# A graph-attention layer on one core: scores and values in 64x64 array tiles, step by step, with a byte mask

## The chip, the cores and the metric

One Trainium2 chip, one core of it. The metric is the device time of one launch in microseconds (us), the median of several runs; less is better. The kernel of before takes 2929.03 us (three runs, 2928.76 to 2929.57).

## What is computed

Eight batches of 2048 nodes with 64 features, one adjacency matrix (2048x2048, int32) for all of them. Cut to what matters:

```
mask = adj + eye(N) > 0
h    = einsum('bnc,hdc->bhnd', x, Wh)                  # 4 heads of 64
def gat(h, b):
    s = where(mask, h @ h^T, -1e16)
    return softmax(s) @ h + b
z    = leaky_relu(concat of heads of gat(h, bh), 0.2)
h2   = z @ Wo^T                                        # back to 64
z2   = leaky_relu(gat(h2, bo), 0.2)
out  = layernorm(x + layernorm(z2) * gamma + beta)
```

All is float32. The kernel takes no maximum: it subtracts one constant shift before the exponential, and a flag computed from all denominators at the end says whether a general version must run again.

## The kernel before

**Units, chunks and steps.** Two attentions run side by side on the 128 partitions: two heads of one batch (a first unit: batch pair `bp`, batch `b2`, head pair `hp`), or the second attention of two batches (a second unit). There are 16 first and 4 second units. A unit is cut into 4 chunks `c` of W = 512 query columns, and a chunk into 16 steps `m`, one for each block of 128 nodes: 20 x 4 x 16 = 1280 steps, 80 chunks.

**One step.** `scores` (L525) makes two matmuls, one for each of the two heads `j`, each with 64 rows and 128 columns of the array (64 features in, 128 nodes out) on 512 columns, into one tile `s` of 128x1024 in PSUM. VectorE (DVE in the rows) subtracts the mask into SBUF (L532), ScalarE (ACT) takes the exponential in place (L534). `values` (L537) makes two more matmuls, each with 128 rows and 64 columns (128 nodes in, 64 features out), which accumulate over the 16 steps into one PSUM bank `o`. GpSimd (POOL) adds the exponentials of steps 0 to 12 into `acc` (`add_up`, L544), and the last three (`DIRECT = 3`) go to TensorE as they are. All matmuls are float32; each shows in the trace as two MATMUL records, its two passes.

**The end of a chunk.** `sums` (L559) adds `acc` and the three direct tiles over the partitions by matmuls with a matrix of ones (`pz`, four array tiles of 32 columns), ScalarE copies the result (`zsb`, L572), DMAs turn it (`zt`), and ScalarE and VectorE apply the leaky ReLU (L582, L583). `invert` (L586) makes the reciprocals on VectorE and spreads them by DMAs (`rd`, `z`), `scale` (L598) multiplies, and `project` (L601) multiplies by Wo (L608) or, in a second unit, by a centring matrix (L616), after which `norm1` and `norm2` (L631, L643) do both normalisations, mostly on VectorE in PSUM.

**The start of a unit.** `prepare` (L498) projects x into `hT` (`ph`, L510; K = 64 rows, 128 columns, one batch at a time) and transposes it into `hN` (`pn`, L520).

**The order.** Every engine runs its instructions in the order in which the program is written. It is written in periods of four steps (`BATCH = 4`): first the four `scores` of a period, then the four `values` of the period before, then the four `add_up`, then the jobs that have been put at this period (`at`, L674). The mask is built in the first periods by 32 jobs (`mask_job`, L682: load, turn into 0 or 1e16 in bf16, transpose, copy).

**Buffers.** PSUM has 8 banks: three score tiles of two banks (`psum`, bufs = 3; the tiles of `pz`, `ph`, `pn` and the mask turn in the same three) and two banks for `o`. There are 14 slots for exponentials and raw loads.

Of the kernel before, what the change touches and what calls it, by code (L numbers as in the profile page):

```python
# [29 lines left out]
BF16 = mybir.dt.bfloat16  # L30
AF = mybir.ActivationFunctionType
# [8 lines left out]
BIG = 1e16  # L40
# [313 lines left out]
def fast_kernel(ctx: ExitStack, tc: tile.TileContext, x, adj, Wh, bh, Wo, bo, gamma, beta, out, flag):  # L354
# [10 lines left out]
    BATCH = 4  # L365
    K = 2 * CB
    DIRECT = 3
# [3 lines left out]
    epool = ctx.enter_context(tc.tile_pool(name="epool", bufs=14))  # L371
    accs = ctx.enter_context(tc.tile_pool(name="accs", bufs=2))
    work = ctx.enter_context(tc.tile_pool(name="work", bufs=7))
    small = ctx.enter_context(tc.tile_pool(name="small", bufs=4))
    psum = ctx.enter_context(tc.tile_pool(name="psum", bufs=3, space=bass.MemoryType.PSUM))
# [9 lines left out]
    def opsum(name):  # L385
        return psum.tile([P, W], F32, tag="o", name=name, bufs=2)

    def wtile(name):
        return work.tile([P, W], F32, tag="w", name=name)

# [5 lines left out]
    identi = const.tile([P, P], I32, name="identi")  # L396
    nc.vector.tensor_copy(identi, ident)
# [21 lines left out]
    zall = const.tile([P, chunks, 8], F32, name="zall")  # L419

# [33 lines left out]

    mask = [const.tile([P, NB, W], BF16, name=f"mask{c}") for c in range(NC)]

# [6 lines left out]
    def mask_rows(c, g, st):  # L463
        if g // 2 == c:
            for k in range(2):
                r = 2 * (g % 2) + k
                d = st[:, r, k * P:(k + 1) * P]
                nc.gpsimd.tensor_tensor(d, d, identi, OP.add)
        m = work.tile([P, CB, 2 * P], BF16, tag="w", name=f"mrow{c}_{g}")
        nc.scalar.activation(m, st, AF.Relu, bias=shifts[:, 2:3], scale=-BIG)  # L470
        return m
# [15 lines left out]

    h2T = {}

    class Unit:  # L490
# [7 lines left out]
        def prepare(self, part):  # L498

            n, h = self.n, part % 2  # L500
            if part < 2:
                if self.second:
                    self.hT = h2T[self.bp]
                    return
                if h == 0:
                    self.hT = big.tile([P, N], F32, tag="hT", name=f"hT{n}")
                rows = slice(self.b2 * C, (self.b2 + 1) * C)
                p = spsum(f"ph{n}_{h}")
                for q in range(2):
                    nc.tensor.matmul(p[:, q * W:(q + 1) * W], whT[rows, self.hp * P:(self.hp + 1) * P],  # L510
                                     xT[self.bp][rows, (2 * h + q) * W:(2 * h + q + 1) * W], start=True, stop=True)
                nc.scalar.copy(self.hT[:, h * 1024:(h + 1) * 1024], p)  # L512
                return

            if h == 0:
                self.hN = big.tile([P, NB, P], F32, tag="hN", name=f"hN{n}")
            p = spsum(f"pn{n}_{h}")
            for k in range(NB // 2):
                m = h * NB // 2 + k
                nc.tensor.transpose(p[:, k * P:(k + 1) * P], self.hT[:, m * P:(m + 1) * P], ident)  # L520
            b = bob.rearrange("p r d -> p (r d)") if self.second else bhb[:, self.hp * P:(self.hp + 1) * P]
            nc.vector.tensor_add(self.hN[:, h * NB // 2:(h + 1) * NB // 2, :], p.rearrange("p (m d) -> p m d", d=P),  # L522
                                 b.unsqueeze(1).to_broadcast([P, NB // 2, P]))

        def scores(self, c, m):  # L525
            ps = spsum(f"s{self.n}_{c}_{m}")
# [10 lines left out]
        def values(self, c, m, e):  # L537
            if m == 0:
                self.O[c] = opsum(f"o{self.n}_{c}")
            for j in range(2):  # L540
                nc.tensor.matmul(self.O[c][j * D:(j + 1) * D, :], self.hN[:, m, j * D:(j + 1) * D], e[:, j, :],  # L541
                                 start=(m == 0), stop=(m == NB - 1))

        def add_up(self, c, m, e):  # L544
# [7 lines left out]
            elif m < NB - DIRECT:  # L552
# [4 lines left out]


        def sums(self, c):  # L559
# [20 lines left out]

            o5 = wtile(f"o5{n}_{c}")
            nc.scalar.mul(o5, self.O[c], SLOPE)  # L582
            nc.vector.tensor_tensor(self.O[c], self.O[c], o5, OP.max)  # L583
            self.zt[c] = zt

        def invert(self, c):  # L586
# [7 lines left out]
            self.z[c] = wtile(f"z{n}_{c}")  # L594
# [3 lines left out]
        def scale(self, c):  # L598
            nc.vector.tensor_tensor(self.z[c], self.O[c], self.z[c], OP.mult)  # L599

        def project(self, c):  # L601

            z, p = self.z[c], self.O[c]
            if not self.second:
                if self.bp not in h2T:
                    h2T[self.bp] = big.tile([P, N], F32, tag="h2T", name=f"h2T{self.bp}")
                rows = slice(self.b2 * D, (self.b2 + 1) * D)
                nc.tensor.matmul(p[rows, :], woT[:, self.hp, :], z, start=True, stop=True)  # L608
                dst = h2T[self.bp][rows, c * W:(c + 1) * W]
                if self.hp == 0:  # L610
                    nc.scalar.copy(dst, p[rows, :])
                else:
                    nc.vector.tensor_add(dst, dst, p[rows, :])  # L613
                return
            for i in range(CB):
                nc.tensor.matmul(p[:, i * P:(i + 1) * P], z[:, i * P:(i + 1) * P],  # L616
                                 centre.rearrange("p r d -> p (r d)"), start=True, stop=True)
            self.norm1(c, p.rearrange("p (k d) -> p k d", d=D))

        def rstd(self, c, y, tag):  # L620

            n = self.n
            st = small.tile([P, 2, K], F32, tag="st", name=f"st{n}_{c}_{tag}")
            sq = wtile(f"sq{n}_{c}_{tag}").rearrange("p (k d) -> p k d", d=D)
            nc.scalar.square(sq, y)  # L625
            nc.vector.tensor_reduce(st[:, 0, :], sq, AX.X, OP.add)  # L626
            nc.scalar.activation(st[:, 1, :], st[:, 0, :], AF.Identity, bias=shifts[:, 3:4], scale=1.0 / D)  # L627
            nc.gpsimd.tensor_tensor(st[:, 0, :], st[:, 1, :], mhalf, OP.pow)  # L628
            return st[:, 0, :].unsqueeze(2).to_broadcast([P, K, D])

        def norm1(self, c, y):  # L631
            xr = wtile(f"xr{self.n}_{c}")
            xv = xr.rearrange("p (i b d) -> p i b d", b=2, d=D)
            for b2 in range(2):
                nc.sync.dma_start(out=xv[:, :, b2, :],
                                  in_=x[2 * self.bp + b2, c * W:(c + 1) * W, :].rearrange("(i p) d -> p i d", p=P))
            nc.vector.tensor_mul(y, y, self.rstd(c, y, 0))
            nc.vector.tensor_mul(y, y, gam.unsqueeze(1).to_broadcast([P, K, D]))
            nc.vector.tensor_add(y, y, bet.unsqueeze(1).to_broadcast([P, K, D]))
            nc.vector.tensor_add(y, y, xr.rearrange("p (k d) -> p k d", d=D))  # L640
            self.xr = xr

        def norm2(self, c):  # L643
            if not self.second:
                return
            y = self.O[c].rearrange("p (k d) -> p k d", d=D)
            mu = small.tile([P, 2, K], F32, tag="mu", name=f"mu{self.n}_{c}")
            nc.vector.tensor_reduce(mu[:, 0, :], y, AX.X, OP.add)
            nc.scalar.mul(mu[:, 1, :], mu[:, 0, :], -1.0 / D)
            nc.vector.tensor_add(y, y, mu[:, 1, :].unsqueeze(2).to_broadcast([P, K, D]))  # L650
            r = self.rstd(c, y, 1)
            nc.vector.tensor_mul(self.xr.rearrange("p (k d) -> p k d", d=D), y, r)
            yv = self.xr.rearrange("p (i b d) -> p i b d", b=2, d=D)
            for b2 in range(2):
                nc.sync.dma_start(out=out[2 * self.bp + b2, c * W:(c + 1) * W, :].rearrange("(i p) d -> p i d", p=P),
                                  in_=yv[:, :, b2, :])
# [3 lines left out]
    for bp in range(B // 2):  # L660
        firsts = [(bp, b2, hp) for b2 in range(2) for hp in range(HP)]
# [6 lines left out]

    PER = NB // BATCH
    periods = [(u, c, q) for u in units for c in range(NC) for q in range(PER)]  # L670
    total = len(periods)
# [24 lines left out]
    for part in range(2):  # L696
        units[0].prepare(part)
# [3 lines left out]
    for part in range(2, 4):  # L701
        units[0].prepare(part)
# [95 lines left out]
```

## Time and profile before

| what | us |
|---|---|
| median of three runs | 2929.03 |
| the profiled execution, its own time | 2929.27 |
| its span in the trace | 2927.8 |
| TensorE busy, share of the span | 2730.6 (93%) |
| GpSimd busy | 2331.8 (80%) |
| VectorE busy | 1799.2 (61%) |
| ScalarE busy | 1656.4 (57%) |
| granted TensorE clock, mean | 0.977 of full speed |

The trace records each instruction with its engine, line and tiles. A busy time of TensorE is not TensorE at its peak: matmuls overlap each other, in different array tiles above all, so how fast it goes is read from the distance of the starts, in the timeline. A row of a timeline merges neighbours of one group: the start, the time from the first start to the last end, and the count; a number in brackets is the idle time ahead of it and what ended it.

### The profile page before, as it was taken

What the parts mean: (1) busy time and instruction counts of PE and PEld (TensorE: products, weight loads), DVE (VectorE), ACT (ScalarE), POOL (GpSimd) and SP (SyncE); (2) the same over time, 40 slices, a digit from 0 to 9 for tenths busy, and PEclk for the clock granted to TensorE, in tenths of its full rate; (3) what the DMA queues carried; (4) which work ended last, traced back from release to release, by engine and by line L of the source; (5) the groups of instructions that cost most, each with busy time, mean ns of one, the idle gap of its engine ahead of it and who ended that gap; (6) DMA issues with size and microseconds to landing.
All of it is one profiled execution on the core that took longest, in us unless ns stands there. A gap on an engine that the chain in (4) does not pass through costs nothing.

```text
span 2927.8 us, 33405 instructions
## 1 busy us (share of the span) xinstructions
PE 2730.6 (93%) x12550; PEld 967.9 (33%) x12550; DVE 1799.2 (61%) x1861; ACT 1656.4 (57%) x1625; POOL 2331.8 (80%) x1025
## 2 busy tenths in 40 slices
PE   7999999999998999999998899999999999998884
PEld 3333333333332333333333233333333333333221
DVE  4666656666666666566666665666566666666564
ACT  5765556556554555655654555565565556555442
POOL 5778888788777887888876888888888888877774
PEclk9999999999999999999999999999999999999997
DMA  4300001000000000100000000010000000000001
GB/s 129 123 16 8 8 8 26 8 8 8 12 22 17 10 9 8 23 8 8 12 18 12 19 8 9 8 26 8 8 8 8 8 8 12 8 12 23 15 19 27
DMA packets 118220, 54.03 MB, mean 18 GB/s; under 512 B 91266, under 2 KB 107714, under 8 KB 118050
## 3 DMA queue, kind: packets, MB, share of 16 engines
q1 hardware_dynamic: 117250, 51.36, 6.6%
q8 instruction: 100, 1.64, 0.2%
q0 software_dynamic: 176, 0.26, 0.1%
q14 instruction: 70, 0.57, 0.1%
q10 hardware_dynamic: 624, 0.20, 0.0%
HBM read 46.60 MB, written 4.52 MB: 17 GB/s over the span
## 4 chain that ended last, share of the span: by engine, by line
PE 60%; ACT 14%; DVE 11%; DMA 5%; issue 4%; SPq 3%; POOL 2%; ACTq 0%; DVEq 0%; POOLq 0%
PE o L541 28%; PE s L529 25%; ACT e L534 11%; DVE e L532 6%; DMA zt<-zsb 4%; SPq L578 3%; PE ph L510 2%; PE o L608 2%; POOL st L628 2%; ACT zsb L572 1%; PE pn L520 1%; ACT o L582 1%; PE pz L569 1%; DVE hN L522 1%; DVE st L626 1%
## 5 line engine op out<-in xcount | busy, mean ns | idle before, releaser
L554 POOL TENSOR_TENSOR acc<-acc,e 128x1024 f32<-128x1024 f32 x880 | 2079.9, 2363 | 79.5 <-ACT e L534 13.0
L534 ACT ACTIVATE e<-e,shifts 128x1024 f32<-128x1024 f32 x1280 | 1452.9, 1149 | 1034.3 <-DVE e L532 1024.6
L532 DVE TENSOR_TENSOR e<-s,mask 128x1024 f32<-128x1024 f32 x1280 | 1475.6, 1215 | 348.2 <-PE s L529 333.0
L541 PE MATMUL o<-e,hN 128*64 128x512 f32 x5120 | 1188.4, 607 | 0.0
L529 PE MATMUL s<-hT 64*128 64x512 f32 x4096 | 1004.3, 609 | 65.7 <-DVE e L532 65.7
L541 PEld LDWEIGHTS o<-e,hN 128*64 128x64 f32 x5120 | 343.5, 138 | 821.3 <-issue 600.9
L529 PEld LDWEIGHTS s<-hT 64*128 64x128 f32 x4096 | 384.1, 187 | 612.0 <-issue 308.0
L550 POOL TENSOR_TENSOR acc<-e,e 128x1024 f32<-128x1024 f32 x80 | 189.8, 2372 | 313.4 <-ACT e L534 313.4
L529 PE MATMUL s<-h2T 64*128 64x512 f32 x1024 | 261.6, 634 | 68.8 <-DVE e L532 50.6
L628 POOL TENSOR_TENSOR st<-st,mhalf 128x8 f32<-128x8 f32 x32 | 52.7, 1647 | 179.2 <-ACT st L627 179.2
L529 PEld LDWEIGHTS s<-h2T 64*128 64x128 f32 x1024 | 95.0, 192 | 215.3 <-DVE e L532 92.2
L583 DVE TENSOR_TENSOR o<-o,o 128x512 f32<-128x512 f32 x80 | 56.0, 700 | 175.8 <-ACT o L582 175.8
L569 PE MATMUL pz<-e,ones 128*32 128x512 f32 x960 | 154.1, 601 | 0.0
L589 DVE TENSOR_REDUCE zall<-zt 128x8 f32<-128x16 f32 x80 | 13.7, 171 | 199.1 <-DMA zt<-zsb 199.0
L569 PE MATMUL pz<-acc,ones 128*32 128x512 f32 x320 | 84.7, 600 | 6.2 <-POOL acc L554 2.2
L599 DVE TENSOR_TENSOR z<-o,z 128x512 f32<-128x512 f32 x80 | 55.2, 690 | 53.5 <-DMA z<-rd 53.4
L512 ACT COPY hT<-ph 128x1024 f32<-128x1024 f32 x32 | 32.4, 1012 | 82.7 <-PE ph L510 82.7
L522 DVE TENSOR_TENSOR hN<-pn,bhb 128x1024 f32<-128x1024 f32 x32 | 39.1, 1223 | 51.8 <-PE pn L520 51.8
L613 DVE TENSOR_TENSOR h2T<-h2T,o 64x512 f32<-64x512 f32 x32 | 21.9, 685 | 76.1 <-PE o L608 76.1
L510 PE MATMUL ph<-xT,whT 64*128 64x512 f32 x128 | 66.6, 644 | 0.0
L608 PE MATMUL o<-z,woT 128*64 128x512 f32 x128 | 65.5, 593 | 0.0
L626 DVE TENSOR_REDUCE st<-sq 128x8 f32<-128x512 f32 x32 | 22.0, 686 | 62.1 <-ACT sq L625 62.1
(68 smaller groups left out, 591.4 us busy)
## 6 DMA issues: line engine op xcount, KB each, us to landing
z<-rd SPq DMA_DIRECT2D x160, 128.0 KB, 2.9
adj<-in_adj_dram SPq DMA_DIRECT2D x32, 512.0 KB, 4.9
zt<-zsb SPq DMA_DIRECT2D x320, 2.0 KB, 1.8
x<-in_x_dram SPq DMA_DIRECT2D x16, 256.0 KB, 4.6
xr<-in_x_dram SPq DMA_DIRECT2D x32, 128.0 KB, 2.9
out_dram<-xr SPq DMA_DIRECT2D x32, 128.0 KB, 2.1
rd<-rt SPq DMA_DIRECT2D x80, 4.0 KB, 1.4
ws<-in_L_gnn_Wh_dram ACTq DMA_DIRECT2D x2, 64.0 KB, 4.3
```

Source lines behind the costliest of these rows:

```text
L510: nc.tensor.matmul(p[:, q * W:(q + 1) * W], whT[rows, self.hp * P:(self.hp + 1) * P], xT[self.bp][rows, (2 * h + q) * W:(2 * h + q + 1) * ...
L522: nc.vector.tensor_add(self.hN[:, h * NB // 2:(h + 1) * NB // 2, :], p.rearrange("p (m d) -> p m d", d=P), b.unsqueeze(1).to_broadcast([P, ...
L529: nc.tensor.matmul(ps[:, j * W:(j + 1) * W], self.hT[rows, m * P:(m + 1) * P], self.hT[rows, c * W:(c + 1) * W], start=True, stop=True)
L532: nc.vector.tensor_tensor(e, ps.rearrange("p (j i) -> p j i", j=2), mask[c][:, m, :].unsqueeze(1).to_broadcast([P, 2, W]), OP.subtract)
L534: nc.scalar.activation(e, e, AF.Exp, bias=shifts[:, 1:2] if self.second else shifts[:, 0:1], scale=1.0)
L541: nc.tensor.matmul(self.O[c][j * D:(j + 1) * D, :], self.hN[:, m, j * D:(j + 1) * D], e[:, j, :], start=(m == 0), stop=(m == NB - 1))
L550: nc.gpsimd.tensor_tensor(acc, self.terms[c][0], e, OP.add)
L554: nc.gpsimd.tensor_tensor(acc, acc, e, OP.add)
L569: nc.tensor.matmul(pz[q:q + 32, :W], ones, terms[s * half + k][:, j, :], start=(k == 0), stop=(k == half - 1), tile_position=(0, q))
L578: nc.sync.dma_start(out=zt[j * D:(j + 1) * D, s, :], in_=zsb[q:q + 1, :].rearrange("o (p k) -> o p k", k=8))
L608: nc.tensor.matmul(p[rows, :], woT[:, self.hp, :], z, start=True, stop=True)
L628: nc.gpsimd.tensor_tensor(st[:, 0, :], st[:, 1, :], mhalf, OP.pow)
```

## The change

The work is the same; its cut and its order are new.

- **Array tiles.** `scores` makes four matmuls of 64 rows x 64 columns (head `j` x half `k` of the 128 nodes) in place of two of 64x128, and `values` four of 64x64 (head `j` x half `r` of the nodes that are summed over) in place of two of 128x64. The two halves `r` accumulate in two PSUM banks, which are added at the end of a chunk: `join` (ScalarE copies one) and `join2` (VectorE adds).
- **Order.** No periods: each step issues the `scores` of step t and then the `values` of step t - 3 (`LAG = 3`), and every job has a step of its own (`LATE`, `NORM`).
- **Buffers.** Two score tiles in place of three, four `o` banks in place of two, 9 slots of exponentials in place of 14, and one tile `eb` for the exponentials of steps 2, 4, 6 and 8.
- **Denominators.** Those four (`BATCH`) are summed by VectorE in four `tensor_reduce` instructions (`reduce`, at steps 13, 14, 15 and 17, each 256 sums over 4 elements that lie 4096 bytes apart). GpSimd adds the other 12 in a first unit, in 11 instructions, and 8 in a second, in 7; a second unit gives its last four to TensorE as they are (`DIRECT = (0, 4)`). So `pz` has 4 matmuls in a first unit and 12 in a second, where it had 8.
- **Mask.** Bytes of 0 and 255 in place of bf16 with 1e16; `offdiag` clears the diagonal after ScalarE.
- **Projections.** `project_x` does both batches of a pair at once in four 64x64 tiles. The product with Wo waits until both head pairs are there (`z0` keeps the first), and does two chunks at once in two column tiles.
- **Normalisation.** Moved from VectorE in PSUM to ScalarE and GpSimd in SBUF (`norm`, eight parts over 16 steps); VectorE keeps two reduces.

```
-    BATCH = 4
-    DIRECT = 3
+    LAG = 3
+    BATCH = (2, 4, 6, 8)
+    DIRECT = (0, 4)
...
-    epool = ctx.enter_context(tc.tile_pool(name="epool", bufs=14))
+    epool = ctx.enter_context(tc.tile_pool(name="epool", bufs=9))
-    psum = ctx.enter_context(tc.tile_pool(name="psum", bufs=3, space=bass.MemoryType.PSUM))
+    psum = ctx.enter_context(tc.tile_pool(name="psum", bufs=2, space=bass.MemoryType.PSUM))
-        return psum.tile([P, W], F32, tag="o", name=name, bufs=2)
+        return psum.tile([P, W], F32, tag="o", name=name, bufs=4)
-    mask = [const.tile([P, NB, W], BF16, name=f"mask{c}") for c in range(NC)]
+    mask = [const.tile([P, NB, W], U8, name=f"mask{c}") for c in range(NC)]
...
         def scores(self, c, m):
-            for j in range(2):
-                rows = slice(j * D, (j + 1) * D)
-                nc.tensor.matmul(ps[:, j * W:(j + 1) * W], self.hT[rows, m * P:(m + 1) * P],
-                                 self.hT[rows, c * W:(c + 1) * W], start=True, stop=True)
+            for k in range(2):
+                for j in range(2):
+                    rows = slice(j * D, (j + 1) * D)
+                    nc.tensor.matmul(ps[k * 64:(k + 1) * 64, j, :], self.hT[rows, m * P + k * 64:m * P + (k + 1) * 64],
+                                     self.hT[rows, c * W:(c + 1) * W], start=True, stop=True)
+            if m == BATCH[0]:
+                self.eb = epool.tile([P, len(BATCH), 2, W], F32, tag="eb", name=f"eb{self.n}_{c}", bufs=1)
...
         def values(self, c, m, e):
             for j in range(2):
-                nc.tensor.matmul(self.O[c][j * D:(j + 1) * D, :], self.hN[:, m, j * D:(j + 1) * D], e[:, j, :],
-                                 start=(m == 0), stop=(m == NB - 1))
+                for r in range(2):
+                    rows = slice(r * 64, (r + 1) * 64)
+                    nc.tensor.matmul(self.O[c][r][j * D:(j + 1) * D, :], self.hN[rows, m, j * D:(j + 1) * D],
+                                     e[rows, j, :], start=(m == 0), stop=(m == NB - 1))
...
+        def reduce(self, c, k):
+            j, i = k // 2, slice(k % 2 * 256, k % 2 * 256 + 256)
+            nc.vector.tensor_reduce(self.part[j][:, i], self.batch[:, :, j, i].rearrange("p k i -> p i k"), AX.X, OP.add)
...
+    LATE = [(19, "join"), (20, "join2"), (20, "sums"), (21, "fifth"), (22, "leaky"), (24, "invert"), (28, "scale"), (30, "project"),
+            (31, "keep")]
+    NORM = [31, 32, 33, 35, 40, 41, 43, 46]
+    for t in range(total + 64):
+        if t < total:
+            u, c, m = steps[t]
+            es[t] = u.scores(c, m)
...
+        if 0 <= t - LAG < total:
+            u, c, m = steps[t - LAG]
+            e = es.pop(t - LAG)
+            u.values(c, m, e)
+            u.add_up(c, m, e)
```

How TensorE's queue moves, at one place in a first unit. Before (`s` the scores, `o` the values; a row `x2` is the two heads):

```order
L529 MATMUL s_1_12_12699<-hT_12116 128x512 x2
L529 MATMUL s_1_13_12705<-hT_12116 128x512 x2
L529 MATMUL s_1_14_12711<-hT_12116 128x512 x2
L529 MATMUL s_1_15_12717<-hT_12116 128x512 x2
L541 MATMUL o_1_12641<-e_1_8_12665,hN_12200 64x512 x2
L541 MATMUL o_1_12641<-e_1_9_12671,hN_12200 64x512 x2
L541 MATMUL o_1_12641<-e_1_10_12677,hN_12200 64x512 x2
L541 MATMUL o_1_12641<-e_1_11_12683,hN_12200 64x512 x2
L608 MATMUL o_0_12469<-z_0_12659,woT 64x512
L529 MATMUL s_2_0_12737<-hT_12116 128x512 x2
```

Now, around step 5 of a chunk, where the four matmuls of `pz` stand; the last two rows come twice, for the two heads, and are followed by the scores of step 6:

```order
L612 MATMUL pz_0_7999<-acc_0_7760,ones 32x512 x2
L612 MATMUL pz_0_7999<-part_0_0_7898,ones 32x512
L612 MATMUL pz_0_7999<-part_0_1_7927,ones 32x512
L537 MATMUL s_1_5_8011<-hT_1_7202 64x512 x4
L552 MATMUL o_1_0_7977<-eb_1_7961,hN_7463 64x512
L552 MATMUL o_1_1_7978<-eb_1_7961,hN_7463 64x512
```

What moved: eight score matmuls and then eight value matmuls have become four and four, and they alternate in every step.

VectorE's queue at the end of a chunk, before (`e` the subtract, `z` the scaling of the chunk before, `hN` the next unit's transposed map):

```order
L532 TENSOR_TENSOR e_2_11_6239<-s_2_11_6236,mask_129 128x1024
L599 TENSOR_TENSOR z_1_6210<-o_1_6020,z_1_6210 128x512
L532 TENSOR_TENSOR e_2_12_6262<-s_2_12_6259,mask_129 128x1024
L532 TENSOR_TENSOR e_2_13_6268<-s_2_13_6265,mask_129 128x1024
L532 TENSOR_TENSOR e_2_14_6274<-s_2_14_6271,mask_129 128x1024
L532 TENSOR_TENSOR e_2_15_6280<-s_2_15_6277,mask_129 128x1024
L522 TENSOR_TENSOR hN_6297<-pn_0_6298,bhb 128x1024
L532 TENSOR_TENSOR e_3_0_6311<-s_3_0_6308,mask_130 128x1024
```

Now, at the same steps of another chunk (`part` the reduces):

```order
L639 TENSOR_TENSOR z0_112<-o6_2_1_7231,z6_2_7595 128x512
L542 TENSOR_TENSOR e6_3_13_7654<-s6_3_13_7649,mask3_131 128x1024
L579 TENSOR_REDUCE part6_3_0_7662<-eb6_3_7479 128x256
L542 TENSOR_TENSOR e6_3_14_7669<-s6_3_14_7664,mask3_131 128x1024
L579 TENSOR_REDUCE part6_3_0_7662<-eb6_3_7479 128x256
L542 TENSOR_TENSOR e6_3_15_7683<-s6_3_15_7678,mask3_131 128x1024
L579 TENSOR_REDUCE part6_3_1_7691<-eb6_3_7479 128x256
L542 TENSOR_TENSOR e7_0_0_7698<-s7_0_0_7693,mask0_128 128x1024
L542 TENSOR_TENSOR e7_0_1_7711<-s7_0_1_7706,mask0_128 128x1024
L579 TENSOR_REDUCE part6_3_1_7691<-eb6_3_7479 128x256
```

What moved: four reduces have come in between the subtracts of steps 12 to 18, three of them in neighbouring steps.

## Rows read from the trace of the kernel before

**Rows 1.** The page's first part: busy time, share of the span, instructions of each engine.

```profile
PE 2730.6 (93%) x12550; PEld 967.9 (33%) x12550; DVE 1799.2 (61%) x1861; ACT 1656.4 (57%) x1625; POOL 2331.8 (80%) x1025
```

**Rows 2.** The page's chain that ended last, shares of the span by engine.

```profile
PE 60%; ACT 14%; DVE 11%; DMA 5%; issue 4%; SPq 3%; POOL 2%; ACTq 0%; DVEq 0%; POOLq 0%
```

**Rows 3.** Timeline of TensorE: start, length, line, tiles, count, [idle before, releaser].

```profile
1570.88 0.62 PE L569 MATMUL pz<-acc,ones 128*32 128x512 f32 x2
...
1571.35 1.46 PE L569 MATMUL pz<-e,ones 128*32 128x512 f32 x10
1572.74 3.65 PE L541 MATMUL o<-e,hN 128*64 128x512 f32 x16
...
1584.53 3.70 PE L529 MATMUL s<-h2T 64*128 64x512 f32 x16
1588.16 3.65 PE L541 MATMUL o<-e,hN 128*64 128x512 f32 x16
1591.75 1.16 PE L616 MATMUL o<-centre,z 128*128 128x128 f32 x8
1592.84 2.85 PE L529 MATMUL s<-hT 64*128 64x512 f32 x12
1600.43 2.08 PE L529 MATMUL s<-hT 64*128 64x512 f32 x4 [4.75 <-DVE e L532]
...
1621.50 1.13 PE L529 MATMUL s<-hT 64*128 64x512 f32 x4 [0.82 <-DVE e L532]
...
1671.40 3.65 PE L541 MATMUL o<-e,hN 128*64 128x512 f32 x16
1674.88 1.02 PE L608 MATMUL o<-z,woT 128*64 128x512 f32 x2
1675.83 3.71 PE L529 MATMUL s<-hT 64*128 64x512 f32 x16
...
1692.24 0.69 PE L510 MATMUL ph<-xT,whT 64*128 64x512 f32 x1
1692.25 0.69 PE L529 MATMUL s<-hT 64*128 64x512 f32 x1
```

**Rows 4.** Timeline of TensorE's weight loads in a block of values.

```profile
2874.76 0.14 PEld L541 LDWEIGHTS o<-e,hN 128*64 128x64 f32 x2 [0.29 <-issue]
...
2876.90 0.14 PEld L541 LDWEIGHTS o<-e,hN 128*64 128x64 f32 x2 [0.29 <-issue]
```

**Rows 5.** Timeline of the start and of the end.

```profile
26.36 2.87 PE L520 MATMUL pn<-ident,hT 128*128 128x128 f32 x16
...
29.16 3.82 PE L529 MATMUL s<-hT 64*128 64x512 f32 x16
...
2878.95 3.65 PE L541 MATMUL o<-e,hN 128*64 128x512 f32 x16
```

**Rows 6.** Timeline of VectorE and GpSimd: instructions in a row without a wait.

```profile
2871.82 4.62 DVE L532 TENSOR_TENSOR e<-s,mask 128x1024 f32<-128x1024 f32 x4 [0.73 <-PE s L529]
...
42.21 19.47 POOL L554 TENSOR_TENSOR acc<-acc,e 128x1024 f32<-128x1024 f32 x8 [0.80 <-ACT e L534]
```

**Rows 7.** Groups by line, shapes apart: busy us, mean ns | idle before, releasers.

```profile
L532 DVE TENSOR_TENSOR e<-s,mask 128x1024 f32<-128x1024 f32 x1280 | 1475.6, 1215 | 348.2 <-PE s L529 333.0 <-POOL acc L554 12.1 <-issue 3.0
...
L626 DVE TENSOR_REDUCE st<-sq 128x8 f32<-128x512 f32 x32 | 22.0, 686 | 62.1 <-ACT sq L625 62.1
...
L589 DVE TENSOR_REDUCE zall<-zt 128x8 f32<-128x16 f32 x80 | 13.7, 171 | 199.1 <-DMA zt<-zsb 199.0
...
L750 DVE TENSOR_REDUCE tot<-zall 128x1 f32<-128x640 f32 x1 | 0.8, 810 | 0.0
...
L397 DVE CAST identi<-ident 128x128 int32<-128x128 f32 x1 | 0.2, 220 | 0.0
L399 DVE TENSOR_SCALAR centre<-ident 128x128 f32<-128x128 f32 x1 | 0.2, 219 | 0.0
...
L751 DVE TENSOR_SCALAR tot<-tot 128x1 f32<-128x1 f32 x1 | 0.1, 144 | 0.0
```

More of the change, by code (lines that the diff above doesn't have):

```diff
@@ L463, in mask_rows @@
     def mask_rows(c, g, st):
+        m = work.tile([P, CB, 2 * P], BF16, tag="w", name=f"mrow{c}_{g}")
+        nc.scalar.activation(m, st, AF.Relu, bias=shifts[:, 2:3], scale=-BIG)
         if g // 2 == c:
@@ L466, in mask_rows @@
                 r = 2 * (g % 2) + k
[L467 to L470, printed above, removed]
+                d = m[:, r, k * P:(k + 1) * P]
+                nc.gpsimd.tensor_tensor(d, d, offdiag, OP.mult)
         return m
@@ L486, in fast_kernel, with project_x @@
     nc.vector.tensor_copy(woT.rearrange("p q d -> p (q d)"), pw[:, 256:256 + HP * D])
+    maps = {}
     h2T = {}
+    held = {}
+    def project_x(bp, hp, q):
+        if q == 0:
+            maps[bp, hp] = big.tile([P, 2, N], F32, tag="hT", name=f"hT{bp}_{hp}")
+        p = spsum(f"ph{bp}_{hp}_{q}").rearrange("p (b i) -> p b i", b=2)
+        for b2 in range(2):
+            rows = slice(b2 * C, (b2 + 1) * C)
+            for j in range(2):
+                nc.tensor.matmul(p[j * D:(j + 1) * D, b2, :], whT[rows, hp * P + j * D:hp * P + (j + 1) * D],
+                                 xT[bp][rows, q * W:(q + 1) * W], start=True, stop=True)
+        nc.scalar.copy(maps[bp, hp][:, :, q * W:(q + 1) * W], p)
     class Unit:
@@ L496, in __init__, with prepare @@
             self.terms, self.zt, self.z, self.O = {}, {}, {}, {}
[L498 to L513, printed above, removed]
+        def prepare(self, h):
+            n = self.n
             if h == 0:
+                self.hT = h2T[self.bp] if self.second else maps[self.bp, self.hp][:, self.b2, :]
                 self.hN = big.tile([P, NB, P], F32, tag="hN", name=f"hN{n}")
@@ L598, in scale @@
         def scale(self, c):
-            nc.vector.tensor_tensor(self.z[c], self.O[c], self.z[c], OP.mult)
+            dst = self.z[c] if self.second or self.hp else z0[:, self.b2, c, :]
+            nc.vector.tensor_tensor(dst, self.O[c][1], self.z[c], OP.mult)
         def project(self, c):
[L603 to L613, printed above, removed]
-                return
@@ L615, in project @@
[L615 to L629, printed above, removed]
@@ L643, in norm2 @@
-        def norm2(self, c):
+            p = self.O[c][0]
+            if self.second:
+                for i in range(CB):
+                    nc.tensor.matmul(p[:, i * P:(i + 1) * P], self.z[c][:, i * P:(i + 1) * P],
+                                     centre.rearrange("p r d -> p (r d)"), start=True, stop=True)
+                return
+            if self.hp == 0 or c % 2 == 0:
+                return
+            if self.bp not in h2T:
+                h2T[self.bp] = big.tile([P, N], F32, tag="h2T", name=f"h2T{self.bp}")
@@ new lines, in project, with keep @@
+            for hp in range(HP):
+                for g in range(2):
+                    k = c - 1 + g
+                    nc.tensor.matmul(p[g * D:(g + 1) * D, :], woT[:, hp, :],
+                                     self.z[k] if hp else z0[:, self.b2, k, :], start=(hp == 0), stop=(hp == HP - 1))
+        def keep(self, c):
+            if self.second or self.hp == 0 or c % 2 == 0:
+                return
+            rows = slice(self.b2 * D, (self.b2 + 1) * D)
+            for g in range(2):
+                k = c - 1 + g
+                nc.scalar.copy(h2T[self.bp][rows, k * W:(k + 1) * W], self.O[c][0][g * D:(g + 1) * D, :])
@@ L644, in norm2, with norm @@
+        def norm(self, c, part):
             if not self.second:
                 return
[L646 to L656, printed above, removed]
+            n = self.n
+            v = lambda t: t.rearrange("p (k d) -> p k d", d=D)
+            row = lambda t: t.unsqueeze(1).to_broadcast([P, K, D])
+            col = lambda t: t.unsqueeze(2).to_broadcast([P, K, D])
@@ L667, in fast_kernel @@
     units = [Unit(n, *o) for n, o in enumerate(order)]
-    PER = NB // BATCH
-    periods = [(u, c, q) for u in units for c in range(NC) for q in range(PER)]
-    total = len(periods)
+    steps = [(u, c, m) for u in units for c in range(NC) for m in range(NB)]
+    total = len(steps)
     jobs = {}
@@ L695, in fast_kernel @@
         transpose_x(0, x0, h)
-    for part in range(2):
-        units[0].prepare(part)
+    for q in range(NC):
+        project_x(0, 0, q)
     for _ in range(3):
@@ L743, in fast_kernel @@
[L743 to L745 removed]
+    assert not jobs
     tot = small.tile([P, 4], F32, tag="tot", name="tot", bufs=1)
```

176 lines of the change are left out of this document (110 added, 66 removed).

## The prediction

> **What bounds the kernel now.** I first read the page's busy shares and its chain, then TensorE's timeline, then the runs of VectorE and GpSimd. TensorE is busy for 93% of the span [rows 1] and holds 60% of the chain that ended last [rows 2]; nothing else holds more than 14%. So I price TensorE's queue, and then ask where it waits.
>
> In the timeline a block of 16 passes is eight rounds of two array tiles that run beside each other. The weight loads of a block of values come in pairs; from the second pair to the last lie five rounds, 2.14 us, 0.428 us a round [rows 4]. `pz` puts four tiles beside each other: its 16 passes take 1.86 us from the first start to the next block's, four rounds and 0.15 [rows 3]. So a round costs the same with two tiles or four.
>
> A block of scores takes 3.63 us to the next start, and a block of values 3.59 (1584.53 to 1588.16 to 1591.75); sixteen rounds are 6.85, so each period pays 0.37 us more. Where values are followed by the product with Wo, of the same 128x64 shape, the block takes 3.48 (1671.40 to 1674.88), and `ph`, of the scores' shape, starts 0.01 us from a score pass [rows 3]. It is thus the change of tile shape that costs, about 0.18 us each.
>
> The rest is waiting. With three score tiles the fourth score matmul of a period waits for VectorE, 0.82 us in one row, and when VectorE is held by a normalisation 4.75 us [rows 3]. By rounds, TensorE's work before is 5120 rounds of scores and values (2191), 320 periods of 0.37 (118), `pz` 320 rounds and a switch each (151), 64 products with Wo of 0.95 (61), `ph` half hidden beside scores (28), and 87 groups of eight transposes, mask turns or centring matmuls of 1.09 (95): 2644. The first scores start at 29 us, and after the last values (2878.95 and eight rounds, 2882.6) the span runs on for 45 [rows 3, 5]. Together 2718 of the span's 2927.8, so about **210 us are waits**. The profiled execution took 2929.27, 0.24 over the median of the three runs.
>
> **The change, part by part.**
>
> *Scores and values.* Twice the matmuls with a quarter of the array each: two rounds of four tiles for the scores of a step and two for its values, 0.856 and 0.856, as before: 2191 us. All are 64x64, so the periods' switches go: -118. No row shows two row tiles times two column tiles. Below, the price cannot fall under a round of 0.428; above, if only two of the four ran together, it doubles. Scores today show two row tiles and `pz` four column tiles, both at the full rate, so I take 0.428.
>
> *`pz`.* 64 first chunks with two rounds and 16 second ones with six: 224 rounds, 96 us; a 32-column shape between 64x64 neighbours costs two switches, 0.37 x 80 = 30: 126, for 151.
>
> *Product with Wo.* 16 groups of four rounds with two switches: 27 + 6 = 33, for 61. *`ph`*: 28 groups of two rounds after the start, 24, without a switch, for 28.
>
> *The 87 groups* now pay two switches instead of one: 1.09 + 0.18, 110, for 95.
>
> TensorE's work: 2191 + 126 + 33 + 24 + 110 = **2484**, 31.0 a chunk.
>
> *VectorE.* A subtract takes 1.135 us when the next follows at once ((4.62 - 1.215)/3) [rows 6, 7]. Its mask is bytes now; a type change alone moved nothing on VectorE (220 against 219 ns) [rows 7], so I add nothing. A reduce of 512 elements took 686 ns and of 640 810 [rows 7], so one of 1024 takes some 1.2 us if the stride of 4096 bytes is free. The strided row is `zall`, 16 elements 32 bytes apart, 171 ns, where one element alone took 144 [rows 7]: at most 27 ns for 16, 1.7 ns each, 1.9 us for 1024. The line through 686 and 810 passes 16 elements at some 205, so the row shows no penalty; I take 1.2 and keep 1.9. A chunk is then 16 x 1.135 + 4 x 1.2 + three passes over 512 elements (join, leaky ReLU, scale; 2.1) + 1.0 for `hN` and the reciprocals: 26 us of 31. Covered on the whole, not in each step: a step is 1.71, a subtract with a reduce 2.335. Steps 13, 14, 15 fall behind by 0.62 each, 16 regains 0.58, 17 loses 0.62: 1.9 in all. With two score tiles a subtract may be late by 1.1 (its scores start at 0, it can begin at 1.1, ends at 2.3, and the tile is written again from 3.4). So TensorE waits 0.8 us a chunk: **60 us**.
>
> *GpSimd.* 11 adds of 2.43 (19.47/8) [rows 6] are 27 us of 31 in a first unit. Six come in neighbouring steps (10 to 15) and lose 0.72 each, so the last ends some 20.6 steps after the chunk's start, where `pz` asks for it at the end of step 20. It just fits; priced at nothing, and if it is late, `pz` holds TensorE's queue and so all scores behind it.
>
> *The rest of the waits.* A unit's two `hN` additions fall behind the last reduce, 0.6 x 20 = 12. ScalarE's copies of `ph` and of x hold a score tile some 0.3 us too long, 34 times, 10. While the mask is built, its copies (bytes from bf16, perhaps twice as long) and 32 loads share slots with the exponentials: 20 allowed. With the 60, 102 us of waits against 210: the normalisation's long ones go, because ScalarE and GpSimd do that work, over 16 steps. Their cover: ScalarE was busy for 1656 us [rows 1], 21 a chunk, and gets about 6 more in second units, whose GpSimd makes only 7 adds. `scale` waits for the DMA of `z`; it comes four steps (6.9 us) after `invert`, as before about, so it is late only if SP's queue is.
>
> *Start and end.* The start keeps its eight cold rounds of `ph`: 29. The end is one chain through the last normalisation, with more and smaller instructions: 45 + 2.
>
> **Sum:** 29 + 2484 + 102 + 47 = 2662 of span; a run lies 1.5 above. I say **2663 us**, 9% less. Without any waits it would be 2561, with as many as now 2772, with reduces at 1.5 us (waits of 2.0 a chunk) 2757. This gives 2570 to 2830.
>
> **Rivals.**
>
> *The strided reduce costs more, and VectorE sets the pace (slower).* At a price r of a reduce the wait is 4r - 4.03 us a chunk (the steps above). 1.9 gives 2888; from r = 2.0 on the kernel is slower than before; at 2.3, twice the contiguous price, it takes 3016. For it: 256 runs of four elements, each 4096 bytes apart, have no row. Against it: `zall`, whose elements are 32 bytes apart [rows 7]. Chance 0.06. [...]
>
> *The four 64x64 tiles don't all run beside each other (slower).* Scores and values would take up to 4382 instead of 2191, and the kernel 4850. Or weights of 64x64 tiles load in the open: 0.14 us [rows 4] in each of 5120 rounds, 3380. `pz` loads four tiles' weights without showing it [rows 3]. Chance 0.03.
>
> *It is not the shape that costs between scores and values.* Then the change does not do what it seems to: the 0.37 would now be paid in each of 1280 steps, 474 us, and the kernel would take 3140. Against: no gap between values and the product with Wo, or between `ph` and scores [rows 3]. Chance 0.01.
>
> *Shallow buffers cost more (faster still).* GpSimd later by 1 to 3 us in each of 64 first chunks, or `scale` waiting for its DMA in most chunks: +64 to +200, up to 2860. Beyond the range with chance 0.06.
>
> **Chances.** My forecast, 2570 to 2830: 0.80. Still fewer waits, below 2570: 0.03. More waits, 2830 to 2923: 0.06. Slower rivals: 0.10. Within 0.2% (what a measurement of this kernel can tell from no change): 0.01. So faster 0.89, same 0.01, slower 0.10.
>
> **What would show it.** Score and value passes in groups of four starts, 0.43 us apart, and no gap between scores and values; a step of 1.71 us. Reduces of 1.2 us; waits of scores on VectorE at steps 17 and 18 of a chunk, under 1 us; no waits of 4 us in second units. GpSimd's last add of a chunk near the start of `pz`. I am wrong if TensorE's starts come two by two, if the reduce takes 2 us, or if `pz` waits for GpSimd by more than 1 us in most chunks.

## The result, and the profile of the changed kernel

| | us |
|---|---|
| before, median of the four runs beside it (2928.76 to 2931.13) | 2929.30 |
| changed, median of four runs (2863.75 to 2865.22) | 2864.74 |
| ratio, with its 95% interval | 0.9778 [0.9761, 0.9795] |
| forecast, and its range | 2663 (2570 to 2830) |
| the profiled execution of the changed kernel, its own time and its span | 2864.34 and 2862.5 |

It is faster by 2.2%, where 9% was forecast: 202 us lie between the forecast and the measurement, and the time is 35 us above the range. In the experiments below, one of the four runs of experiment 4 took 4801.74 us at a mean granted clock of 0.694, where the other three have 0.983 to 0.985, and is left out of its median. The page's first part, against [rows 1], and the chain's shares by line:

```profile
PE 2566.9 (90%) x22534; PEld 851.8 (30%) x22534; DVE 2410.8 (84%) x2117; ACT 1771.7 (62%) x2089; POOL 2074.0 (72%) x961
...
PE s L537 9%; PE o L552 8%; DVE part L579 7%; DVE e L542 6%; POOL acc L567 2%; PE pz L612 2%; DVE eb L542 1%; ACT e L543 1%; DVE z L639 1%; ACT xr L705 0%; DVE hN L529 0%; PE pn L527 0%; POOL st L709 0%; DMA z<-rd 0%; ACT hT L508 0%
```

VectorE went from 61% to 84% of the span, 612 us more, and its reduces (L579) stand in the chain almost as long as either of TensorE's two main lines (the chain covers 43% of the span only, so this is a hint and no account of the whole). TensorE's timeline, read as [rows 3], first with `pz` of a second unit, then where nothing disturbs it, then around the end of a chunk:

```profile
1508.52 1.04 PE L552 MATMUL o<-e,hN 64*64 64x512 f32 x8
1509.49 0.62 PE L612 MATMUL pz<-acc,ones 128*32 128x512 f32 x2
...
1512.20 1.09 PE L537 MATMUL s<-h2T 64*64 64x512 f32 x8
1513.11 1.04 PE L552 MATMUL o<-eb,hN 64*64 64x512 f32 x8
1513.97 1.04 PE L537 MATMUL s<-h2T 64*64 64x512 f32 x8
1514.83 1.04 PE L552 MATMUL o<-e,hN 64*64 64x512 f32 x8
1515.68 1.04 PE L537 MATMUL s<-h2T 64*64 64x512 f32 x8
...
1537.48 1.09 PE L527 MATMUL pn<-ident,hT 128*128 128x128 f32 x8 [1.09 <-DVE e L542]
1539.20 1.09 PE L537 MATMUL s<-h2T 64*64 64x512 f32 x8 [0.62 <-DVE e L542]
...
1542.21 1.09 PE L537 MATMUL s<-h2T 64*64 64x512 f32 x8 [1.06 <-DVE hN L529]
```

Scores and values follow each other by 0.86 us, a step by 1.71: the rounds and the missing switch are as forecast. What is not as forecast is the wait on VectorE. Its timeline in the same stretch:

```profile
1527.11 1.21 DVE L542 TENSOR_TENSOR e<-s,mask 128x1024 f32<-128x1024 f32 x1
1528.24 1.97 DVE L579 TENSOR_REDUCE part<-eb 128x256 f32<-128x1024 f32 x1
1530.14 1.21 DVE L542 TENSOR_TENSOR e<-s,mask 128x1024 f32<-128x1024 f32 x1
1531.27 1.99 DVE L579 TENSOR_REDUCE part<-eb 128x256 f32<-128x1024 f32 x1
1533.18 1.20 DVE L542 TENSOR_TENSOR e<-s,mask 128x1024 f32<-128x1024 f32 x1
```

A subtract and a reduce together come every 3.03 us (1527.11, 1530.14, 1533.18), where TensorE's step takes 1.71; no row of these has a wait. Groups by line, shapes apart, as [rows 7]:

```profile
L542 DVE TENSOR_TENSOR e<-s,mask 128x1024 f32<-128x1024 f32 x960 | 1165.8, 1220 | 265.4 <-PE s L537 248.1 <-POOL acc L567 13.9 <-ACT e L543 0.5
...
L579 DVE TENSOR_REDUCE part<-eb 128x256 f32<-128x1024 f32 x320 | 637.0, 1991 | 0.0
...
L628 DVE TENSOR_REDUCE zall<-zt 128x8 f32<-128x16 f32 x80 | 12.7, 159 | 0.3 <-DMA zt<-zsb 0.3
```

The subtract with its byte mask takes what it took before (1220 against 1215 ns). The reduce takes **1991 ns** where the sum had 1.2 us.

### The profile page after: what moved, and what is told of

Read it like the earlier page. It is cut to its first block, busy times and chain, and to the rows that moved or that the text cites. A ratio compares the mean times of both kernels' runs of the same rounds, so it can differ in the third digit from the quotient of the medians.

```text
span 2862.5 us, 53599 instructions
## 1 busy us (share of the span) xinstructions
PE 2566.9 (90%) x22534; PEld 851.8 (30%) x22534; DVE 2410.8 (84%) x2117; ACT 1771.7 (62%) x2089; POOL 2074.0 (72%) x961
## 5 line engine op out<-in xcount | busy, mean ns | idle before, releaser
L567 POOL TENSOR_TENSOR acc<-acc,e 128x1024 f32<-128x1024 f32 x736 | 1743.3, 2369 | 513.2 <-ACT e L543 477.6
L543 ACT ACTIVATE e<-e,shifts 128x1024 f32<-128x1024 f32 x960 | 1098.6, 1148 | 798.1 <-DVE e L542 796.4
L542 DVE TENSOR_TENSOR e<-s,mask 128x1024 f32<-128x1024 f32 x960 | 1165.8, 1220 | 265.4 <-PE s L537 248.1
L537 PE MATMUL s<-hT 64*64 64x512 f32 x8192 | 1087.3, 601 | 159.9 <-DVE e L542 103.8
L552 PE MATMUL o<-e,hN 64*64 64x512 f32 x7680 | 999.7, 591 | 1.9 <-ACT e L543 1.9
L579 DVE TENSOR_REDUCE part<-eb 128x256 f32<-128x1024 f32 x320 | 637.0, 1991 | 0.0
L543 ACT ACTIVATE eb<-eb,shifts 128x1024 f32<-128x1024 f32 x320 | 367.7, 1149 | 214.7 <-DVE eb L542 213.1
L542 DVE TENSOR_TENSOR eb<-s,mask 128x1024 f32<-128x1024 f32 x320 | 391.7, 1224 | 92.8 <-PE s L537 82.4
L552 PEld LDWEIGHTS o<-e,hN 64*64 64x64 f32 x7680 | 292.7, 133 | 537.7 <-issue 454.3
L552 PE MATMUL o<-eb,hN 64*64 64x512 f32 x2560 | 333.8, 592 | 0.0
```

Of the source, the lines that this page charges most:

```text
L537: nc.tensor.matmul(ps[k * 64:(k + 1) * 64, j, :], self.hT[rows, m * P + k * 64:m * P + (k + 1) * 64], self.hT[rows, c * W:(c + 1) * W], st ...
L542: nc.vector.tensor_tensor(e, ps, mask[c][:, m, :].unsqueeze(1).to_broadcast([P, 2, W]), OP.subtract)
L543: nc.scalar.activation(e, e, AF.Exp, bias=shifts[:, 1:2] if self.second else shifts[:, 0:1], scale=1.0)
L552: nc.tensor.matmul(self.O[c][r][j * D:(j + 1) * D, :], self.hN[rows, m, j * D:(j + 1) * D], e[rows, j, :], start=(m == 0), stop=(m == NB - 1))
L567: nc.gpsimd.tensor_tensor(acc, acc, e, OP.add)
L579: nc.vector.tensor_reduce(self.part[j][:, i], self.batch[:, :, j, i].rearrange("p k i -> p i k"), AX.X, OP.add)
```

## The experiments

The theory after the result: the price of the reduce is the whole error. Its rivals: VectorE's load as such, however it is made up; the order of the reduces; GpSimd. Times of one run have no interval. The runs of before beside the experiments have medians of 2930.6 to 2931.6.

**1. The same reduces on neighbouring elements** (lines shortened). They add the wrong elements, so the denominators are not the layer's; so that nothing overflows, the shift before the exponential is larger and ScalarE adds a constant where it copies `pz`.

```
-  tensor_reduce(part, batch[:, :, j, i].rearrange("p k i -> p i k"))
+  flat = batch.rearrange("p a b i -> p (a b i)")[:, k * 1024:(k + 1) * 1024]
+  tensor_reduce(part, flat.rearrange("p (i k) -> p i k", k=4))
```

> The change, but each reduce adds four neighbouring elements of the same tile in place of four that lie 4096 bytes apart (the denominators are wrong; a constant is added to them on ScalarE and the shift before the exponential is larger, so that nothing overflows). Same counts, same steps. Theory 1 (the distance between the elements makes the reduce dear, and that alone is what the forecast missed): a reduce takes 1.2 us in place of 1.99, and the kernel 2640 to 2700. Rival 2 (256 short rows of four elements are what costs, wherever they lie): 1.99 us, 2865. Rival 3 (the reduce is cheaper, but the shallow buffers hold the kernel anyway): 1.2 us, over 2780.

Measured: 2665.75 us (one run), 199 less than the changed kernel. Its group of reduces:

```profile
L581 DVE TENSOR_REDUCE part<-eb 128x256 f32<-128x1024 f32 x320 | 386.9, 1209 | 0.0
```

With a reduce of 1209 ns the kernel takes what was forecast with 1.2 us, to 3 us. So the error is the price of these 320 instructions, and the rest of the sum holds as a whole.

**2. Where the price changes.** The four reduces of a chunk read elements 8, 16, 32 and 256 bytes apart (lines shortened; the denominators are wrong again, with the same shift and constant):

```
+  k == 0: flat.rearrange("p (a k b) -> p a b k", k=4, b=2)
+  k == 1: ... b=4;   k == 2: ... b=8;   k == 3: ... b=64
```

> [...] Theory 1: 8 bytes near 1.2 us, a jump at one distance, the farther ones 1.99; the kernel between the run with neighbours and 2865. Rival 2: all four 1.99, 2865.

Measured: 2812.18 us (one run). The groups, in the order 8, 16, 32, 256 bytes (L582, L584, L586, L588):

```profile
L584 DVE TENSOR_REDUCE part<-eb 128x256 f32<-128x1024 f32 x80 | 161.1, 2014 | 0.0
L588 DVE TENSOR_REDUCE part<-eb 128x256 f32<-128x1024 f32 x80 | 159.0, 1987 | 0.0
L586 DVE TENSOR_REDUCE part<-eb 128x256 f32<-128x1024 f32 x80 | 159.0, 1987 | 0.0
...
L582 DVE TENSOR_REDUCE part<-eb 128x256 f32<-128x1024 f32 x80 | 96.7, 1209 | 0.0
```

At 8 bytes nothing is paid; from 16 on the price is whole and the distance no longer matters. The price is 0.76 ns an element ((1987 - 1209) / 1024). L586 has the 32 bytes of `zall`: by this price, an estimate, the 16 elements of that row would pay 12 ns of its 171 (16 x 0.76), too little to see, as the mean of the same instruction moved by as much between the two kernels (171 and 159).

**3. The reduces apart**, at steps 10, 12, 14 and 16 in place of 13, 14, 15 and 17 (strided, as in the changed kernel).

> The change with its four reduces at steps 10, 12, 14 and 16 of a chunk in place of 13, 14, 15 and 17; the output is right. Theory 1 with the backlog of the forecast's working (a step is 1.717, a subtract 1.135, a reduce 1.9): eight steps fall behind by 3.6 in place of 4.7 us, 1.1 is free, so 1.1 us a chunk comes back: 2780. Rival (VectorE's load in a chunk decides, not where it lies): 2865 within 10.

Measured: 2838.59 us (2837.36 to 2840.50, four runs), 0.9686 [0.967, 0.9702] of before: 26 us better than the changed kernel, where 85 were expected. A single wait for VectorE became shorter in the mean (the longest did not), but there were more of them (a part of each lies beside matmuls that still run: where the first row of this run below has 474.5 us, the matmuls themselves wait 179.7). In the view of waits (total us, times, longest) of the weight loads ahead of TensorE, the changed kernel has

```profile
PEld s L537 <- DVE e L542: 315.4, 281, 2.6
PEld s L537 <- DVE eb L542: 141.4, 134, 2.2
```

and this one

```profile
PEld s L537 <- DVE e L542: 474.5, 504, 3.7
...
PEld s L537 <- DVE eb L542: 60.8, 106, 0.8
```

The way of counting that the prediction used, a backlog that only the reduces build up, is too simple. VectorE's timeline here has collisions that it leaves out: the reduce of step 12 behind the scaling, the one of step 16 behind a reduce of the normalisation that itself waits for ScalarE. What such a collision costs these rows do not say; experiments 8 and 9 come back to it.

```profile
1482.19 0.69 DVE L690 TENSOR_REDUCE st<-sq 128x8 f32<-128x512 f32 x1 [1.06 <-ACT sq L680]
1482.80 1.91 DVE L579 TENSOR_REDUCE part<-eb 128x256 f32<-128x1024 f32 x1
...
1508.91 0.68 DVE L639 TENSOR_TENSOR z<-o,z 128x512 f32<-128x512 f32 x1
1509.51 1.96 DVE L579 TENSOR_REDUCE part<-eb 128x256 f32<-128x1024 f32 x1
```

**4. No reduces at all.** In a first unit GpSimd adds 13 steps, as before the change, and three blocks go to TensorE as they are; in a second unit it adds nine, and seven go (lines shortened).

```
-  BATCH = (2, 4, 6, 8); DIRECT = (0, 4); epool bufs=9, and eb
+  BATCH = ();           DIRECT = (3, 7); epool bufs=13
```

> The change without its part on VectorE: no reduces and no tile for them; GpSimd adds steps 0 to 12 in a first unit and three go to TensorE (steps 0 to 8 and seven in a second), 13 slots; the output is right. Theory 1: TensorE gets 160 more rounds (69 us), VectorE's backlog is gone, 42 us of other waits stay: 2670. Rival (GpSimd sets the pace: 12 adds of 2.43 are 29.2 us of a chunk of 31.9, and the sums wait for it): 2750 or more, with waits of pz on the adds of some us in most first chunks.

Measured: 2680.67 us (2680.08 to 2682.34, three runs), 0.915 [0.9132, 0.9168] of before, 11 us above the expectation. The part of the change that gave VectorE a share of the denominators thus costs 184 us as it is written. All the rest of the change, with TensorE's longer `pz`, is worth 250 us. TensorE is at 96% of the span and VectorE at 68%:

```profile
PE 2581.1 (96%) x23174; PEld 896.6 (33%) x23174; DVE 1833.2 (68%) x1797; ACT 1785.2 (67%) x2089; POOL 2266.3 (85%) x1041
```

**5. The old tile shapes in the new order** (on experiment 4: scores 64x128, values 128x64 into one bank, no join; lines shortened).

```
-  for k in range(2): for j in range(2): matmul(ps[64k:64k+64, j], hT[rows j, 64 nodes], ...)
+  for j in range(2): matmul(ps[:, j], hT[rows j, 128 nodes], ...)
```

> e4_no_batch with the tile shapes of the kernel before in the new alternating order: scores as two matmuls of 64x128, values as two of 128x64 into one bank, and no join of halves. The theory says that a change of tile shape costs TensorE about 0.18 us and that the alternating order pays two of them in each of 1280 steps: 474 us more than e4's 2682, about 3150 us, with a step of 2.08 us in TensorE's timeline and gaps between scores and values. The rival says that the shape costs nothing and that before lost its 0.37 us a period otherwise: then it stays at e4's 2682 (a little less, since VectorE and ScalarE lose the join).

Measured: 3029.64 us (one run), 349 above experiment 4 and slower than before. TensorE's timeline:

```profile
1507.41 1.08 PE L547 MATMUL o<-e,hN 128*64 128x512 f32 x4
1508.42 1.13 PE L536 MATMUL s<-h2T 64*128 64x512 f32 x4
1509.48 1.08 PE L547 MATMUL o<-e,hN 128*64 128x512 f32 x4
```

The step is 2.07 us (1507.41 to 1509.48), 0.36 above 1.71: two switches of 0.18, as the theory said. That is 0.36 x 1280 = 461 us of TensorE's queue, and the total rose by 112 less. A part of this is seen: VectorE now has time (it waits 1100 us for scores in this run), TensorE stands idle for 54 us of the span (3027.9 less 2974.0 busy) where experiment 4 has 98 (2678.9 less 2581.1), and its mean granted clock is 0.994 for 0.985. How the rest divides was not measured. The claim that it is the change of shape that costs, and that 64x64 tiles end it, is shown; in the alternating order the old shapes cost more (349 us) than the change without its reduces gains (250 us).

**6. Additions in place of reduces.** VectorE adds blocks 2 and 4, then 6, then 8, as whole tiles at steps 7, 9 and 11; the other engines' shares are those of the changed kernel (in words, not code).

```
-  four tensor_reduce, 128x256 <- 128x1024 (strided)
+  three tensor_tensor: part = e2 + e4; part += e6; part += e8   (128x1024)
```

> The four blocks on VectorE again, as three additions of whole tiles (2+4, then 6, then 8, at steps 7, 9 and 11) in place of four strided reduces; 12 slots, no eb tile; GpSimd and TensorE have the same share of the denominators as in the changed kernel. Theory 1 (the reduce's price was the whole error) says: an addition of 128x1024 takes about 1.2 us like a subtract, 3.6 us a chunk where the reduces took 8.0, no two in neighbouring steps, so VectorE hardly falls behind: TensorE's work as in the changed kernel, 70 us below e4's, waits of some 50, about 2625 us, below e1's 2666 and e4's 2682. Rival: VectorE and GpSimd, which both read two operands from SBUF now, hold each other up: the additions take 2 us or more, or GpSimd's 2.4 us grow, pz waits for acc, and it takes 2700 to 2850 us.

Measured: 2701.77 us (2701.19 to 2704.65, five runs), 0.922 [0.9207, 0.9232]: a miss of 77, on the rival's side. The groups:

```profile
L565 POOL TENSOR_TENSOR acc<-acc,e 128x1024 f32<-128x1024 f32 x736 | 1808.9, 2458 | 326.5 <-ACT e L541 285.0 <-POOL acc L565 0.2
...
L574 DVE TENSOR_TENSOR part<-part,e 128x1024 f32<-128x1024 f32 x160 | 236.3, 1477 | 0.0
L574 DVE TENSOR_TENSOR part<-e,e 128x1024 f32<-128x1024 f32 x80 | 114.0, 1425 | 0.0
...
L606 PE MATMUL pz<-acc,ones 128*32 128x512 f32 x320 | 87.6, 627 | 56.3 <-POOL acc L565 56.2
```

In one stretch, VectorE's timeline has

```profile
1498.63 1.90 DVE L574 TENSOR_TENSOR part<-e,e 128x1024 f32<-128x1024 f32 x1
...
1503.58 2.70 DVE L574 TENSOR_TENSOR part<-part,e 128x1024 f32<-128x1024 f32 x1
...
1508.47 1.21 DVE L574 TENSOR_TENSOR part<-part,e 128x1024 f32<-128x1024 f32 x1
```

and GpSimd's

```profile
1497.08 8.12 POOL L565 TENSOR_TENSOR acc<-acc,e 128x1024 f32<-128x1024 f32 x3
```

GpSimd's three additions end at 1505.20; VectorE's addition, begun at 1503.58, ends 1.08 us after that, at 1506.28. It seems to have done nothing until GpSimd was through; the next one, with no addition of GpSimd beside it, took 1.21. And GpSimd needed 8.12 us for three additions, where its mean of 2369 in the changed kernel gives 7.1. By these rows the two engines take turns, and GpSimd, which had no room, comes late for `pz` (56 us, 16 in the changed kernel). Whether additions at other steps than 7, 9 and 11 would collide less was not run.

**7. The four blocks stored two by two.** Element by element, block 2 beside block 4 and 6 beside 8, so that a reduce finds two of its elements on 8 neighbouring bytes (lines shortened).

```
-  eb = [P, 4, 2, W];     e = eb[:, k];                   reduce batch[:, :, j, i] as "p k i -> p i k"
+  eb = [P, 2, 2, W, 2];  e = eb[:, k // 2, :, :, k % 2]; reduce batch[:, :, j, i, :] as "p q i r -> p i q r"
```

> [...] The subtract, the exponential and the values read or write these four blocks with elements 8 bytes apart. [...] Rival 2 (the 8-byte stride costs the others instead): subtracts or exponentials of these four blocks of 1.6 us or more, or value passes that take more than 0.43 us a round, TensorE 0.43 us more for each of 5120 such matmuls in rounds of four at the worst, 2900 or more.

Measured: 2676.72 us (2675.76 to 2677.79, five runs), 0.913 [0.9118, 0.9143], where some 2666, as in experiment 1, were expected. The groups that touch these blocks:

```profile
L543 ACT ACTIVATE eb<-eb,shifts 128x1024 f32<-128x1024 f32 x320 | 402.7, 1258 | 164.9 <-DVE eb L542 158.1
L542 DVE TENSOR_TENSOR eb<-s,mask 128x1024 f32<-128x1024 f32 x320 | 396.3, 1238 | 102.2 <-PE s L537 92.0
L579 DVE TENSOR_REDUCE part<-eb 128x256 f32<-128x1024 f32 x320 | 386.7, 1208 | 0.0
```

The reduce costs 1208 ns while it adds the right four blocks: what counts is that its elements come in neighbouring pairs, not that all four are neighbours. ScalarE pays 0.11 us for each of these exponentials (1149 in the changed kernel). TensorE pays too, in its timeline:

```profile
1524.47 1.07 PE L552 MATMUL o<-eb,hN 64*64 64x512 f32 x8
1525.38 1.02 PE L537 MATMUL s<-hT 64*64 64x512 f32 x8
1526.23 1.02 PE L552 MATMUL o<-e,hN 64*64 64x512 f32 x8
1527.09 1.02 PE L537 MATMUL s<-hT 64*64 64x512 f32 x8
```

Values from `eb` take 0.91 us to the next start here, from other tiles 0.86 (in the changed kernel 0.86 for both, 1513.11 to 1513.97 above); over the whole trace the usual distance is 0.90. Some 0.04 us in each of 320 blocks are, as an estimate, 13 us, about what this kernel takes more than experiment 1 (11 us).

**8 and 9. The cheap reduces at other steps**: 10, 12, 14, 16, and then 10, 13, 15, 17.

> The same with the reduces at steps 10, 12, 14 and 16, as in the third experiment. By the prediction's own way of counting, a step with a reduce falls behind by 0.62 us at 1.2 us and the next one regains 0.58, so hardly anything piles up and the wait of 0.8 us a chunk goes: about 2620 us. Rival: VectorE's other work (join, leaky ReLU, scale, hN) decides when scores are late, and the place of cheap reduces does not matter: as the run beside it, within 10 us.

> The pairs layout again, with the reduces at steps 10, 13, 15 and 17: each with a step between, and none at step 12, where VectorE scales the chunk before. In the trace of the run with 10, 12, 14 and 16, the reduce at 12 stands right behind the scaling (a subtract pair, 0.68 and 1.21 us in a row), and in second units the one at 16 stands behind a reduce of the normalisation that waits 1.6 us for ScalarE. If what is left of the waits on VectorE comes from such collisions, this gives 2640 to 2650 us; if the place no longer matters, it stays within 5 us of 2655.

Measured: 2655.33 us (2653.49 to 2656.48, five runs), 0.9056 [0.9044, 0.9069], and **2637.92 us** (2636.44 to 2640.93, five runs), **0.8997 [0.8985, 0.901]**, both against before. The first is 35 us above its expectation (experiment 3 was 59 above its own): in its timeline the collisions of step 12 and step 16 are there with cheap reduces too. The second, which avoids them, gains 17 us more, a little over its 5 to 15; as it moves three reduces at once, this does not say what each collision cost. Of TensorE's waits on VectorE and GpSimd these are left:

```profile
PE pz L612 <- POOL acc L567: 24.7, 6, 6.9
PE s L537 <- DVE e L542: 14.9, 22, 1.3
```

This version differs from the changed kernel by the layout of one tile and four numbers, and takes 227 us less (2637.92 against 2864.74); it is the fastest of all that were run. TensorE is busy for 96% of its span; the next limit is GpSimd's `acc`, which holds `pz` by up to 6.9 us where a second unit ends. Such a wait costs more than itself, as TensorE's timeline shows:

```profile
1496.09 1.07 PE L612 MATMUL pz<-acc,ones 128*32 128x512 f32 x2 [6.90 <-POOL acc L567]
...
1497.95 1.99 PE L537 MATMUL s<-hT 64*64 64x512 f32 x8
1499.71 1.93 PE L552 MATMUL o<-eb,hN 64*64 64x512 f32 x8
1501.42 1.24 PE L537 MATMUL s<-hT 64*64 64x512 f32 x8
```

The scores behind the wait take 1.76 us to the next start and the values 1.71, where they otherwise take 0.86 and 0.90.

## Why the prediction was wrong

- **The failed step is the price of the reduce**: "I take 1.2 and keep 1.9". It is 1.99 us. Of the rows that bore on it, the prediction drew a line through two reduces of contiguous elements and found that `zall` [rows 7] lay below it, hence no penalty. But the line's fixed part (some 190 ns) is more than all of `zall` takes: it doesn't hold for so short an instruction. The other reading of the same row, 144 ns for one element and 1.7 ns for each of the 16, gave 1.9, and that was right to 5%, but by luck: in the changed kernel the same instruction took 159 ns (L628 above), from which the same reading gives 0.9 ns an element and 1.1 us. The row cannot tell 1.2 from 1.9. No row of before priced a stride over as many elements, and with that left open the forecast should not have rested on the lower end.
- **The wait that follows from it** was written as 4r - 4.03 us a chunk. It gives 64 us at the 1.209 of experiment 1, where the total came out right, and 314 at 1.99, which would be 2917 in all; measured were 2865. The extra 0.78 us of each of 320 reduces is 250 us, and 199 of them reached the end. So the slope was too steep, and the point from which the kernel would be slower than before lies above 2.0. While TensorE waits for VectorE, GpSimd catches up (`pz` waits 16.0 us for `acc` in the changed kernel, 24.3 in experiment 1), but that is 8 of the 51 us; where the others went stays open.
- **The range and the chances** kept 1.9 in words ("keep 1.9") but not in numbers: the rival of the dearer reduce had 0.06 and was counted among the slower ones, though at 1.9 its own sum gave 2888, which is faster than before. (Its other bound, "twice the contiguous price", is 2.4 by the prediction's 1.2, not 2.3.) With equal weight on both bounds the range would have reached beyond 2865.
- **The 210 us called waits** hold more than waits, which the prediction did not read. In [rows 3] the four passes behind the wait of 4.75 us take 2.08 us, those behind 0.82 take 1.13: from 1600 to 1602 us the granted clock is 0.50, and the block of values that follows takes 5.04 us for 3.65. By the mean granted clocks, 0.977 before and 0.988 in the changed kernel, some 135 and 69 us lie at 0.50, an estimate that takes all the rest at 1.00 and includes the idle end. So the long waits of the normalisation took more with them than themselves when they went.
- **Scores and values, 2191 and no switch**: right (0.86 and 0.86; experiment 5 has the switches back, 0.18 each). The two rivals on the tiles fell.
- **`pz`**: the rounds are right; around it are 0.25 us, not 0.37 (1508.52 to 1509.49, and six rounds and 0.14 to 1512.20). Some 10 us too much.
- **The byte mask at nothing**: right, 1220 ns. While it is built, its copies take 1219 ns each for 690.
- **GpSimd "just fits"**: right for the changed kernel to 16.0 us in four waits, where VectorE sets the pace; in the faster versions it is the next limit (24.7 us in experiment 9).
- **Start and end**: the eight rounds of `ph` at the start take 5.20 us for 7.19, the first scores come at 27.8 for 29, and from the last values to the end 45 for 47.

The rest of the sum held well enough that experiment 1, with the reduce at the assumed price, came within 3 us. That shows the sum as a whole, not each small wait in it: those for `hN`, copies and the mask were not measured one by one, and errors among them may cancel.

## What to carry to other kernels

When a change gives an engine a new access pattern, look for a row of that pattern that is long enough to show a price; where there is none, or the rows give two prices, let the range hold both with real weight. Before work is moved to an engine with spare time, add it up step by step beside everything else that stands there in the same steps, since a burst on an engine that is 84% busy is paid by the one that waits. Where a reduce must run over blocks that lie apart, storing the blocks two by two so that two of its operands are neighbours can bring back the contiguous price (here 1208 ns for 1991) at a small cost to the writers (0.11 us for each of ScalarE's exponentials).

## What the runs showed that was not expected

- A VectorE reduce of 1024 float32 elements has two prices, 1209 ns with neighbours up to 8 bytes apart and 1987 to 2014 from 16 bytes on; beyond that the distance (32, 256, 4096 bytes) changes nothing.
- Neighbouring pairs are enough even if the next two elements lie 8192 bytes on (1208 ns, experiment 7); the writers and readers of such a block pay little: ScalarE's exponential in place 1258 ns for 1149, TensorE's two rounds of values some 0.90 us for 0.86.
- A VectorE addition with both inputs in SBUF took from 1.21 to 2.70 us in one stretch, and GpSimd's additions rose from 2369 to 2458 ns in the mean, while the subtract, which reads PSUM and SBUF, stayed at 1216 ns beside the same GpSimd.
- Behind a wait of several microseconds TensorE was slower for a few microseconds of work: before the change, behind one of 4.75 us, the granted clock stood at 0.50 until 1605 us; in experiment 9, behind one of 6.9 us, values and scores took 1.71 and 1.76 us where they otherwise take 0.90 and 0.86.
